# Diagonal matrices of B: made on ScalarE, or fetched from zeros kept in DRAM through ScalarE's own DMA queue

## The chip, the cores and the metric

The kernel runs on one core of one Trainium2 chip. The core has five engines that work side by side, each through its own list of instructions in order: TensorE (PE, matrix products), VectorE (DVE), ScalarE (ACT, functions of single elements and copies), GpSimd (POOL) and SyncE (SP, which here only asks for DMA transfers). Sixteen DMA engines move the data between DRAM and the on-chip memory SBUF. TensorE writes its results to a second on-chip memory, PSUM. The metric is the device time of one execution in microseconds (us). Before the change it is 22,061.91 us, the median of three runs (22,050.39 to 22,083.94).

## The reference: what is computed

Four layers run one after the other on x of shape (4, 64, 64, 128) in float32. Layers 0, 1 and 3 are vision state space layers; layer 2 is a gated block without a scan. Almost all the time goes into the scan of the three state space layers. Cut to what matters, such a layer is:

```python
xz = _ln(input) @ in_proj_w;  x_, z = split(xz)          # 256 channels each
xc = silu(depthwise_conv3x3(x_) + conv_b)                 # B, 256, 64, 64
x0, x1 = rows of xc, columns of xc                        # two orders of the 4096 positions
xs = stack([x0, x1, x0 reversed, x1 reversed])            # K = 4 directions
dts, Bs, Cs = split(einsum('bkdl,kcd->bkcl', xs, x_proj_w), [8, 24])   # R = 8, N = 16, N = 16
delta = softplus(einsum('bkrl,kdr->bkdl', dts, dt_w) + dt_b)
A = -exp(A_log)                                           # K, 256, 16
def step(h, t):                                           # over the 4096 positions
    h = exp(d_t[..., None] * A) * h + (d_t * x_t)[..., None] * B_t[:, :, None, :]
    return h, einsum('bkdn,bkn->bkd', h, C_t)
ys = scan(step) + Ds * xs
y = sum of the four directions, each put back in order
x = input + (_ln(y) * silu(z)) @ out_proj_w
return x + (gelu(_ln(x) @ fc1_w + fc1_b) @ fc2_w + fc2_b)
```

The term (d_t x_t) B_t is what the change touches. For each state n of 16, channel and position it is the product du = delta x of that channel and position with B[n] of that position. B[n] is the same for all channels.

## The kernel before

**Turns, chunks, periods.** Twelve turns (four images, three state space layers) follow one another. A turn has 4 directions of 8 chunks of 512 positions, so there are 384 chunks. Channels lie on the 128 partitions, positions along the rows, and the 256 channels are two halves m. The 16 states are four groups q of CQ = 4. A chunk is worked in eight periods i, one for each pair of group q = i // 2 and half m. There are 3,072 periods.

**A period.** The loop body from L985 on writes the order by hand; nothing reorders it. For its four states a period does four scans on VectorE (L924), each over 512 positions, with the decays da = exp(delta A) from ScalarE (`decay`, L908, for the following period). The input of the scans comes in two ways. The first two states of a group get theirs from TensorE: `pair_db` (L895) multiplies du, transposed to positions on partitions, with a matrix that has B of each position on its diagonal, two states interleaved. The result stands in PSUM as dbp, which has one buffer. The other two states get theirs on VectorE: `lift` (L915) lets ScalarE copy du to PSUM, and L1048 and L1049 multiply it with bb, rows of B that a DMA has spread over all partitions. POOL multiplies the states with C (`times_c`, L936, rows cb spread by DMA), TensorE adds the products up (`add_up`, L951), and ScalarE saves the last states (`save`, L932).

**The diagonals.** `diagonals` (L885) makes the matrices on ScalarE, one half of a group in each period: four activations on the 128 x 128 identity with a column of bt as scale (L891). They are for the group two ahead, or the next chunk's. The tile diag has two buffers of 4 x 128 x 128 x 2 numbers on 128 partitions, 512 KB each. bt is B transposed, from four TensorE transposes (L851) and a ScalarE copy (L856).

**The prologue.** `prologue` (L814) prepares the next chunk in pieces, cut at each `yield`; PIECES says at which half periods the next piece runs: number 2i in the middle of period i, 2i + 1 at its end. The pieces load xs and, for the two reversed directions, xd; project xs to xd (80 rows of dts, B and C for two directions, L835 and L837); project dts to delta (L842, L845) and apply softplus (L847, with loads of function tables); transpose B; store xd to DRAM (L854); form du on POOL (L859) and transpose it (L865, L867).

**SyncE's queue.** All DMA requests are SyncE's, in the order of the program: `spread` (L870) for bb and cb each group, xs, xd, the store of xd, and those of the interleaved steps. A request waits on SyncE until its buffer is free.

**The other layers' work.** `between` makes lists of small steps: output norm, gate, projections, MLP, norms, convolution, and the gated layer. `other` (L1008) puts them into four places of each period, by a planner that spreads their cost (`ROOM`, `cost`, `when`) over a turn. `convolve` and `silu` end in stores of the convolved image to DRAM: x_row by rows (L477) and x_col by columns, the latter in 128 x 64 runs of eight numbers (L472).

Of the kernel before, what the change touches and what calls it, by code (L numbers as in the profile page):

```python
# [13 lines left out]
F32 = mybir.dt.float32  # L14
AF = mybir.ActivationFunctionType
# [7 lines left out]
DI, N, R, K = 256, 16, 8, 4  # L23
NX = R + 2 * N
HID = 4 * C
CH = 512
NCH = L // CH
RPC = CH // W
P = 128
WP = W + 2  # L30

CQ = 4

PAIRED = (0, 2, 4, 6)


PIECES = (0, 3, 4, 6, 8, 9, 10, 11, 12, 13)


_VSS = [  # L40
# [58 lines left out]
def vss_stack_kernel(ctx: ExitStack, tc: tile.TileContext, x: bass.AP, weights, out: bass.AP, n_batch=B, layers=(0, 1, 2, 3)):  # L99
# [6 lines left out]
    nc = tc.nc  # L106

    const = ctx.enter_context(tc.tile_pool(name="const", bufs=1))
    keep = ctx.enter_context(tc.tile_pool(name="keep", bufs=1, space=DRAM))

    ident = const.tile([P, P], F32, name="ident")
# [14 lines left out]
    for i in layers:  # L126
# [14 lines left out]
        t = const.tile([P, small_n + VSS_N - tail_at], F32, name=f"w{i}")  # L141
# [27 lines left out]
    def cols(c):  # L169
        return slice(c * CH, (c + 1) * CH)  # L170
# [13 lines left out]
    y_sb = const.tile([P, 2, L], F32, name="y_sb")  # L184
# [574 lines left out]
        return [S[a:z] for a, z in zip([0] + marks[1:], marks[1:] + [len(S)])]  # L759


    turns = []
    for e in range(0, n_batch, 2):
        for i in (0, 1, 3):
# [2 lines left out]
    for turn, (e, i) in enumerate(turns):  # L767

        for nth, k in enumerate((1, 3, 0, 2) if turn else (0, 1, 3, 2)):
            for ci in range(NCH):  # L770
                s = SimpleNamespace(turn=turn, e=e, v=wt[i], layer=i, nth=nth, k=k, ci=ci)
                s.c = NCH - 1 - ci if k >= 2 else ci
                s.columns, s.back = k % 2 == 1, k >= 2
                s.end = 0 if s.back else CH - 1
                s.step = slice(None, None, -1 if s.back else 1)
                s.first, s.last = ci == 0, ci == NCH - 1
                s.flip = len(chunks) % 2
                s.diag, s.cb, s.bb, s.h, s.hc = {}, {}, {}, {}, {}
                chunks.append(s)
    per_turn = K * NCH  # L780

# [27 lines left out]
    def scans(pool, ring, deep, psum):  # L809
# [4 lines left out]
        def prologue(s):  # L814


            lane, v = lanes[s.e % 2], s.v
            s.xs = ring.tile([P, 2, CH], F32, tag="xs", name="xs")
            nc.sync.dma_start(out=s.xs, in_=(lane.x_col if s.columns else lane.x_row)[:, :, cols(s.c)])
            if s.first:  # L820
                s.dt = pool.tile([R, DI], F32, tag="dt", name="dt_w")
                nc.sync.dma_start(out=s.dt, in_=weights[s.layer][1][:, s.k * DI : (s.k + 1) * DI])


            s.xd_d = lane.xd[s.k % 2][s.c]
            s.xd = pool.tile([2 * NX, CH], F32, tag="xd", name="xd")
            if s.back:
                nc.sync.dma_start(out=s.xd[:NX], in_=s.xd_d[1])
            yield
            if s.back:  # L830
                yield
            else:
                ps = psum.tile([P, CH], F32, tag="misc", name="ps_x")
                for m in range(2):
                    nc.tensor.matmul(ps[: 2 * NX], v["xp"][:, s.k % 2, m, :], s.xs[:, m], start=(m == 0), stop=(m == 1))  # L835
                yield
                nc.scalar.copy(s.xd, ps[: 2 * NX])  # L837
            s.delta = pool.tile([P, 2, CH], F32, tag="delta", name="delta")
            halves = (s.flip, 1 - s.flip)
            for m in halves:  # L840
                ps = psum.tile([P, CH], F32, tag="misc", name="ps_dt")
                nc.tensor.matmul(ps, s.dt[:, m * P : (m + 1) * P], s.xd[:R], start=True, stop=True)  # L842
                yield
                func = AF.Identity if m == halves[0] else AF.Softplus
                nc.scalar.activation(s.delta[:, m], ps, func, bias=v["dtb"][:, s.k, m : m + 1])  # L845
            m = halves[0]
            nc.scalar.activation(s.delta[:, m], s.delta[:, m], AF.Softplus)  # L847
            nc.scalar.preload_act_table_set("natural_log_exp_and_others")
            ps = psum.tile([P, 4, NX], F32, tag="misc", name="ps_bt")
            for j in range(4):  # L850
                nc.tensor.transpose(ps[:, j, :], s.xd[:NX, j * P : (j + 1) * P], ident[:NX, :NX])  # L851
            yield
            if not s.back:
                nc.sync.dma_start(out=s.xd_d.rearrange("k r t -> (k r) t"), in_=s.xd)  # L854
            s.bt = pool.tile([P, 4, N], F32, tag="bt", name="bt")
            nc.scalar.copy(s.bt, ps[:, :, R : R + N])  # L856
            s.du = pool.tile([P, 2, CH], F32, tag="du", name="du")
            for m in halves:
                nc.gpsimd.tensor_mul(s.du[:, m], s.delta[:, m], s.xs[:, m])  # L859
                yield  # L860
            s.duT = pool.tile([P, 4, 2, P], F32, tag="duT", name="duT")
            for m in halves:
                ps = psum.tile([P, 4, P], F32, tag="misc", name="ps_duT")
                for j in range(4):
                    nc.tensor.transpose(ps[:, j, :], s.du[:, m, j * P : (j + 1) * P], ident)  # L865
                yield
                nc.scalar.copy(s.duT[:, :, m, :], ps)  # L867
            yield

        def spread(s, q, b):  # L870

            rows_of, at, count = ((s.bb, CQ * q + 2, CQ - 2), (s.cb, CQ * q, CQ))[b]
            rows_of[q] = pool.tile([P, count, CH], F32, tag="bc"[b] + "b", name="bc"[b] + "b")
            row = R + b * N + at
            nc.sync.dma_start(
                out=rows_of[q], in_=s.xd_d[s.k // 2 : s.k // 2 + 1, row : row + count].to_broadcast([P, count, CH])
            )
# [4 lines left out]
            q = i // 2  # L882
            return q, (i + q + s.flip) % 2

        def diagonals(s, q, half):  # L885

            if half == 0:
                s.diag[q] = pool.tile([P, 4, P, 2], F32, tag="diag", name="diag")
            for t in (2 * half, 2 * half + 1):
                for j in range(2):  # L890
                    nc.scalar.activation(  # L891
                        s.diag[q][:, t, :, j], ident, AF.Copy, scale=s.bt[:, t, CQ * q + j : CQ * q + j + 1]
                    )

        def pair_db(s, i):  # L895
            q, m = place(s, i)
# [6 lines left out]
        def decay(s, i, side):  # L903
            q, m = place(s, i)
            da = ring.tile([P, 2, CH], F32, tag="da", name="da")
            for j in range(2):
                n = CQ * q + 2 * side + j
                nc.scalar.activation(da[:, j], s.delta[:, m], AF.Exp, scale=s.v["a"][:, s.k, m, n : n + 1])  # L908
            return da
# [5 lines left out]
        def lift(s, i):  # L915
            nc.scalar.copy(dv[i % 2], s.du[:, place(s, i)[1]])  # L916
# [17 lines left out]
        def times_c(s, i, side):  # L934
            hc = s.hc[i, side] = deep.tile([P, 2, CH], F32, tag="hc", name="hc")
            nc.gpsimd.tensor_mul(hc, s.h[i, side], s.cb[i // 2][:, 2 * side : 2 * side + 2, :])  # L936
            if side == 1 and i in PAIRED:
                nc.gpsimd.tensor_add(hc, hc, s.hc[i, 0])  # L938

        def add_up(s, i, *calls):  # L940
# [4 lines left out]
            for call in calls:  # L945
                opens = i == start and call == (2 if i in PAIRED else 0)
                if opens:
# [21 lines left out]
        for step in sum([combine(0, psums)] + opening[:4], []):  # L969
            step()  # L970
        s = chunks[0]
        pro = prologue(s)
        for _ in pro:
            pass
        for q, half in ((0, 0), (0, 1), (1, 0)):
            diagonals(s, q, half)
        spread(s, 0, 0)
        spread(s, 0, 1)
        pair_db(s, 0)
# [5 lines left out]
        for at, (s, i) in enumerate(periods):  # L985
            then = periods[at + 1] if at + 1 < len(periods) else None
            if i == 0:
                nxt = chunks[at // 8 + 1] if at // 8 + 1 < len(chunks) else None
                if nxt:
                    pro, nxt.dt = prologue(nxt), s.dt  # L990
                s.state = pool.tile([P, 2, N], F32, tag="state", name="state") if s.first else before[0].state
                if at % (8 * per_turn) == 0:
                    segments = [
                        SimpleNamespace(todo=steps, done=0, dense=True, total=len(steps), frm=frm, to=to)

                        if to - frm <= 4 * 8
                        else SimpleNamespace(
                            todo=steps, done=0, dense=False, total=sum(map(cost, steps)), frm=when(frm), to=when(to)
                        )
                        for steps, frm, to in meanwhile(s.turn)  # L1000
                    ]

            def piece(number):

                if nxt and number in PIECES:
                    next(pro)
# [34 lines left out]
            other(1)  # L1041
            if spreads:
                spread(*spreads, 1)
            if then:
                da_next[1] = decay(*then, 1)
            save(s, i, 0)
# [6 lines left out]
            times_c(s, i, 1)  # L1053
            if then:
                lift(*then)

            q, half = (i + 2 + i % 2) // 2, 1 - i % 2
            if q < 4:
                diagonals(s, q, half)
            elif nxt:  # L1060
                diagonals(nxt, q - 4, half)
            if i < 2 and full:
                leave(*full.pop(0))
            if before:
# [107 lines left out]
```

## Time and profile before

One profiled execution took 22,072.22 us; its span is 22,070.4 us and the granted TensorE clock was 0.963 of full speed.

| What | From the page |
|---|---|
| TensorE matmuls | 19,694.9 us, 89% of the span |
| VectorE | 19,479.8 us, 88% |
| GpSimd | 19,266.5 us, 87% |
| ScalarE | 18,587.9 us, 84% |
| Diagonals on ScalarE (L891) | 12,288 activations, 3,952.1 us |
| B transposed: TensorE (L851), ScalarE copy (L856) | 170.5 us, 73.6 us |
| SyncE's DMA queue | 2,436,336 packets, 3,046.22 MB, 44.4% of 16 engines' span |
| DMA, all queues | mean 139 GB/s |

A line of the groups names the line of the kernel, the engine, the operation, out<-in by tile names with shapes, and the count; behind the bar stand busy us, mean ns of one, and the idle time just before them with what ended it. A line of the waits names the engine, line and tile that waited, and for what; then us in total, times and the longest. A timeline line has start, length (both us), engine, line, operation and out<-in; SPq is SyncE's queue of requests, and a length there is how long SyncE was held by the request, not how long the transfer took. A line of the view by windows has the stretch, its length, busy us (and instructions) of PE, PEld (weight loads), DVE, ACT and POOL, the granted clock, the mean busy share of the 16 DMA engines, and GB/s.

### The profile page before, as it was taken

The page shows a single profiled execution, that of the slowest core. Times are in us where ns is not written, and L with a number is a line of the kernel's source. Part 1 is how long each engine was busy: PE and PEld are TensorE (multiplying, and loading weights), DVE is VectorE, ACT ScalarE, POOL GpSimd, SP SyncE. Part 2 cuts the span into 40 slices and gives each one's busy share as a digit, 9 for nine tenths or more (in the row PEclk, how much of TensorE's full clock was granted, in tenths as well). Part 3 has the DMA queues.
Part 4 walks back from the last instruction along what each step waited for, and adds up shares of the span by engine and source line. Part 5 has one row for each costly group of instructions (what it writes and reads, how often), then busy time and mean ns, then how long its engine had stood idle before and what let it go on. Part 6 is the DMA issues. An engine that isn't in the chain of part 4 may idle for free. (4 is left out here: it accounts for less than half of the span.)

```text
span 22070.4 us, 216982 instructions
## 1 busy us (share of the span) xinstructions
PE 19694.9 (89%) x58234; PEld 10511.8 (48%) x58234; DVE 19479.8 (88%) x20186; ACT 18587.9 (84%) x40022; POOL 19266.5 (87%) x8862
## 2 busy tenths in 40 slices
PE   7898998898889889889989988989988988898897
PEld 3444444444444444444444444444444444444443
DVE  5999999999888888899889899989988888889996
ACT  6888888888888888888888888888888888888887
POOL 5999899899888888888889888988988888889996
PEclk9999999999999999999999999999999999999999
DMA  4444444444335434434534544444443453354342
GB/s 109 147 149 146 135 144 149 136 139 151 130 131 139 142 128 140 146 133 145 144 138 144 145 141 140 141 147 134 142 149 127 137 143 137 131 140 145 140 144 101
DMA packets 2437559, 3060.10 MB, mean 139 GB/s; under 512 B 1753840, under 2 KB 1790064, under 8 KB 2238192
## 3 DMA queue, kind: packets, MB, share of 16 engines
q1 hardware_dynamic: 2436336, 3046.22, 44.4%
q8 instruction: 472, 7.73, 0.1%
q14 instruction: 751, 6.15, 0.1%
HBM read 2784.41 MB, written 261.49 MB: 138 GB/s over the span
## 5 line engine op out<-in xcount | busy, mean ns | idle before, releaser
L936 POOL TENSOR_TENSOR hc<-h,cb 128x1024 f32<-128x1024 f32 x6144 | 14399.4, 2363 | 2276.5 <-DVE h L924 1113.1
L951 PE MATMUL yp<-hc,ident 128*128 128x512 f32 x18432 | 9062.1, 618 | 688.3 <-POOL hc L938 546.8
L908 ACT ACTIVATE da<-delta,w 128x512 f32<-128x512 f32 x12288 | 8148.0, 713 | 543.5 <-DVE h L924 530.5
L924 DVE TENSOR_TENSOR_SCAN h<-da,state,dbp 128x512 f32<-128x512 f32 x5376 | 6573.3, 1262 | 818.9 <-PE dbp L899 576.0
L899 PE MATMUL dbp<-diag,duT 128*128 128x256 f32 x24576 | 6012.6, 388 | 652.4 <-DVE h L924 560.1
L924 DVE TENSOR_TENSOR_SCAN h<-da,state,dv 128x512 f32<-128x512 f32 x5376 | 6589.4, 1264 | 0.0
L899 PEld LDWEIGHTS dbp<-diag,duT 128*128 128x128 f32 x24576 | 4675.2, 193 | 2921.3 <-issue 1673.1
L951 PEld LDWEIGHTS yp<-hc,ident 128*128 128x128 f32 x18432 | 3483.6, 196 | 4999.1 <-issue 3656.8
L891 ACT ACTIVATE diag<-ident,bt 128x128 f32<-128x128 f32 x12288 | 3952.1, 402 | 0.0
L938 POOL TENSOR_TENSOR hc<-hc 128x1024 f32<-128x1024 f32 x1536 | 3624.1, 2359 | 120.4
L1048 DVE TENSOR_TENSOR dv<-dv,bb 128x512 f32<-128x512 f32 x3072 | 2088.3, 680 | 945.9 <-ACT dv L916 730.3
L916 ACT COPY dv<-du 128x512 f32<-128x512 f32 x3072 | 1799.1, 586 | 984.6 <-DVE h L924 977.1
L1049 DVE TENSOR_TENSOR dv<-dv,bb 128x512 f32<-128x512 f32 x3072 | 2118.4, 690 | 0.0
L444 PE MATMUL gap<-halo,cw 128*128 128x512 f32 x3456 | 1750.8, 604 | 5.9 <-DVE cen L281 2.2
L924 DVE TENSOR_TENSOR_SCAN h<-da,dbp 128x512 f32<-128x512 f32 x768 | 891.1, 1202 | 250.7 <-PE dbp L899 166.9
L859 POOL TENSOR_TENSOR du<-delta,xs 128x512 f32<-128x512 f32 x768 | 979.9, 1276 | 31.8 <-ACT delta L847 31.8
L842 PE MATMUL ps_dt<-xd,dt_w 8*128 8x512 f32 x1536 | 881.2, 654 | 130.2 <-ACT delta L845 78.2
L932 ACT COPY state<-h 128x2 f32<-128x2 f32 x5376 | 964.3, 179 | 0.0
L444 PEld LDWEIGHTS gap<-halo,cw 128*128 128x128 f32 x3456 | 628.1, 191 | 654.8 <-issue 617.8
L924 DVE TENSOR_TENSOR_SCAN h<-da,dv 128x512 f32<-128x512 f32 x768 | 893.8, 1204 | 0.0
L845 ACT ACTIVATE delta<-ps_dt,w 128x512 f32<-128x512 f32 x768 | 524.9, 683 | 103.0 <-PE ps_dt L842 98.2
L865 PEld LDWEIGHTS ps_duT<-ident,du 128*128 128x128 f32 x3072 | 383.7, 142 | 321.9 <-issue 255.8
(122 smaller groups left out, 11686.6 us busy)
## 6 DMA issues: line engine op xcount, KB each, us to landing
cb<-xd_d SPq DMA_DIRECT2D x1536, 1024.0 KB
bb<-xd_d SPq DMA_DIRECT2D x1536, 512.0 KB
xs<-x_row_d SPq DMA_DIRECT2D x192, 512.0 KB
xs<-x_col_d SPq DMA_DIRECT2D x192, 512.0 KB
x_col_d<-down SPq DMA_DIRECT2D x192, 256.0 KB
x_row_d<-wide SPq DMA_DIRECT2D x96, 512.0 KB
y_d<-y_sb SPq DMA_DIRECT2D x96, 512.0 KB
y<-y_d SPq DMA_DIRECT2D x96, 512.0 KB
```

Source lines behind the costliest of these rows:

```text
L444: nc.tensor.matmul(z.ps, z.cw[:, m, t, :], z.halo[c][:, dy : dy + RPC, dx : dx + W], start=(t == 0), stop=(t == 8),)
L859: nc.gpsimd.tensor_mul(s.du[:, m], s.delta[:, m], s.xs[:, m])
L891: nc.scalar.activation(s.diag[q][:, t, :, j], ident, AF.Copy, scale=s.bt[:, t, CQ * q + j : CQ * q + j + 1])
L899: nc.tensor.matmul(s.db[:, t * P : (t + 1) * P, :], s.duT[:, t, m, :], s.diag[q][:, t], start=True, stop=True)
L908: nc.scalar.activation(da[:, j], s.delta[:, m], AF.Exp, scale=s.v["a"][:, s.k, m, n : n + 1])
L916: nc.scalar.copy(dv[i % 2], s.du[:, place(s, i)[1]])
L924: nc.vector.tensor_tensor_scan(s.h[i, side][:, j, s.step], da[:, j, s.step], db[:, s.step], init, ALU.mult, ALU.add)
L936: nc.gpsimd.tensor_mul(hc, s.h[i, side], s.cb[i // 2][:, 2 * side : 2 * side + 2, :])
L938: nc.gpsimd.tensor_add(hc, hc, s.hc[i, 0])
L951: nc.tensor.matmul(getattr(s, f"yp{m}"), ident, s.hc[i, side][:, j], start=opens, stop=closes)
L1048: nc.vector.tensor_mul(db, du, s.bb[i // 2][:, 0])
L1049: nc.vector.tensor_mul(du, du, s.bb[i // 2][:, 1])
```

## The change

B's diagonal matrices are no longer computed. Two regions of DRAM, one for even and one for odd chunks, are filled with zeros at the start. A region has, for each of the four groups, 512 rows of DIAG = 258 numbers, one row for each position. Once xd of a chunk is there, ScalarE asks for two DMA transfers (j = 0, 1) that write B of the group's first two states into columns 0 and 1 of the rows of all positions: 4 x 512 single numbers each, 258 apart. The reader takes the same memory as rows of 256 numbers instead of 258 (129 rows to each 128 positions, the last left out). Read so, position p's two numbers stand at columns 2p and 2p + 1 of row p: a diagonal. `diagonals` becomes one DMA load of 512 KB for a whole group, also asked for by ScalarE, in the middle of every odd period, for the group that TensorE needs two periods on. The transposes of B and bt go. The store of xd moves from the piece at number 9 to a new piece at number 5, together with the two transfers; the identity and the second product for delta move to number 7. There is one piece more.

```diff
+DIAG = 2 * P + 2
-PIECES = (0, 3, 4, 6, 8, 9, 10, 11, 12, 13)
+PIECES = (0, 3, 4, 5, 7, 8, 9, 10, 11, 12, 13)
...
+    diag_d = []
+    zero = y_sb.rearrange("p m l -> p (m l)")[:, : N // CQ * 4 * DIAG]
+    nc.vector.memset(zero, 0.0)
+    for j in range(2):
+        diag_d.append(keep.tile([N // CQ, CH * DIAG], F32, name=f"diag_d{j}"))
+        nc.sync.dma_start(
+            out=diag_d[j].rearrange("q (p c) -> p q c", p=P), in_=zero.rearrange("p (q c) -> p q c", q=N // CQ)
+        )
...
                 s.flip = len(chunks) % 2
+                s.diag_d = diag_d[s.flip]
...
                 yield
                 nc.scalar.copy(s.xd, ps[: 2 * NX])
+            yield
+            if not s.back:
+                nc.sync.dma_start(out=s.xd_d.rearrange("k r t -> (k r) t"), in_=s.xd)
+            rows = s.diag_d.rearrange("q (t c) -> q t c", c=DIAG)
+            for j in range(2):
+                nc.scalar.dma_start(out=rows[:, :, j], in_=s.xd[R + j : R + N : CQ])
...
             nc.scalar.preload_act_table_set("natural_log_exp_and_others")
-            ps = psum.tile([P, 4, NX], F32, tag="misc", name="ps_bt")
-            for j in range(4):
-                nc.tensor.transpose(ps[:, j, :], s.xd[:NX, j * P : (j + 1) * P], ident[:NX, :NX])
             yield
-            if not s.back:
-                nc.sync.dma_start(out=s.xd_d.rearrange("k r t -> (k r) t"), in_=s.xd)
-            s.bt = pool.tile([P, 4, N], F32, tag="bt", name="bt")
-            nc.scalar.copy(s.bt, ps[:, :, R : R + N])
...
-        def diagonals(s, q, half):
-
-            if half == 0:
-                s.diag[q] = pool.tile([P, 4, P, 2], F32, tag="diag", name="diag")
-            for t in (2 * half, 2 * half + 1):
-                for j in range(2):
-                    nc.scalar.activation(
-                        s.diag[q][:, t, :, j], ident, AF.Copy, scale=s.bt[:, t, CQ * q + j : CQ * q + j + 1]
-                    )
+        def diagonals(s, q):
+            s.diag[q] = pool.tile([P, 4, P, 2], F32, tag="diag", name="diag")
+            nc.scalar.dma_start(
+                out=s.diag[q].rearrange("p t c n -> p t (c n)"),
+                in_=s.diag_d[q].rearrange("(t p c) -> p t c", t=4, c=2 * P)[:P],
+            )
...
-        for q, half in ((0, 0), (0, 1), (1, 0)):
-            diagonals(s, q, half)
+        for q in range(2):
+            diagonals(s, q)
...
             if spreads:
                 spread(*spreads, 1)
+
+            if i % 2:
+                q = i // 2 + 2
+                if q < 4:
+                    diagonals(s, q)
+                elif nxt:
+                    diagonals(nxt, q - 4)
             if then:
                 da_next[1] = decay(*then, 1)
...
             if then:
                 lift(*then)
-
-            q, half = (i + 2 + i % 2) // 2, 1 - i % 2
-            if q < 4:
-                diagonals(s, q, half)
-            elif nxt:
-                diagonals(nxt, q - 4, half)
```

## The prediction, made before the changed kernel had run

> **What bounds the kernel now.** The page's first part was read first, to see whether one engine sets the time.
>
> ```profile
> PE 19694.9 (89%) x58234; PEld 10511.8 (48%) x58234; DVE 19479.8 (88%) x20186; ACT 18587.9 (84%) x40022; POOL 19266.5 (87%) x8862
> ```
>
> None does. Four engines are 84 to 89% busy and wait for one another, so the groups come next, for what ScalarE would lose and what a chunk costs at least.
>
> ```profile
> L936 POOL TENSOR_TENSOR hc<-h,cb 128x1024 f32<-128x1024 f32 x6144 | 14399.4, 2363 | 2276.5 <-DVE h L924 1113.1
> L908 ACT ACTIVATE da<-delta,w 128x512 f32<-128x512 f32 x12288 | 8148.0, 713 | 543.5 <-DVE h L924 530.5
> L891 ACT ACTIVATE diag<-ident,bt 128x128 f32<-128x128 f32 x12288 | 3952.1, 402 | 0.0
> L938 POOL TENSOR_TENSOR hc<-hc 128x1024 f32<-128x1024 f32 x1536 | 3624.1, 2359 | 120.4
> L859 POOL TENSOR_TENSOR du<-delta,xs 128x512 f32<-128x512 f32 x768 | 979.9, 1276 | 31.8 <-ACT delta L847 31.8
> ```
>
> Over 384 chunks POOL's three groups are 49.5 us a chunk. On VectorE four scans and two products take about 6.2 us a period, 49.6 us a chunk. The span gives 57.5 us a chunk, so some 8 us a chunk are lost to waits. The starts of the scans (L924) in the trace give the mean length of periods 0 to 7: 7.57, 7.31, 7.20, 7.21, 7.41, 7.29, 6.38, 6.46 us. Periods 3 to 5 last 21.9 us together where 18.6 would do: 3.3 us of the loss lies there.
>
> The list of waits says how much of it is ScalarE being late.
>
> ```profile
> ACT dv L916 <- DVE h L924: 977.1, 1124, 4.0
> DVE h L924 <- PE dbp L899: 742.8, 557, 8.6
> DVE dv L1048 <- ACT dv L916: 730.3, 328, 7.5
> POOL hc L936 <- DMA cb<-xd_d: 406.8, 81, 13.0
> DVE dv L1048 <- DMA bb<-xd_d: 196.1, 64, 6.3
> DVE h L924 <- ACT da L908: 104.7, 62, 16.8
> ```
>
> VectorE waits 730.3 + 104.7 = 835 us for ScalarE, 2.2 us a chunk; as often ScalarE is ahead (977 us). Relief of ScalarE is worth at most about that.
>
> Last, what a DMA request costs the engine that makes it: SyncE's own timeline.
>
> ```profile
> 10249.75 0.37 SPq L472 DMA_DIRECT2D x_col_d<-down  x1
> 10250.17 4.50 SPq L477 DMA_DIRECT2D x_row_d<-wide  x1
> 10254.76 0.55 SPq L875 DMA_DIRECT2D cb<-xd_d  x1
> 10255.35 1.02 SPq L472 DMA_DIRECT2D x_col_d<-down  x1
> 10256.47 8.50 SPq L327 DMA_DIRECT2D xt<-in_x  x1
> ```
>
> A request takes 0.3 to 0.5 us, but one made just after the x_col store is held 4.5 us. That store is 128 x 64 runs of 32 bytes, 8,192 pieces. In the trace all 108 requests that directly follow one are held, 4.48 us at the least, 4.54 in the middle. The view by windows shows why:
>
> ```profile
> 10251.00:10252.00 1.00, 0.33 (x1) 0.29 (x2) 1.00 (x2) 1.00 (x3) 1.00 (x1) 1.00 0.76 54
> 10252.00:10253.00 1.00, 1.00 (x3) 0.28 (x2) 0.88 (x1) 1.00 (x2) 0.77 (x1) 1.00 0.76 54
> ```
>
> The last column is GB/s: 54 GB/s in 32-byte pieces are 1.7 pieces a ns, one per 9.4 ns on each of 16 engines, and the next request goes out when most of the 512 pieces of each engine are handed out. SyncE computes nothing, so this costs little today.
>
> **The change, part by part.**
>
> *Taken from ScalarE*: 32 diagonal activations a chunk. The timeline shows four in 1.28 us, so 10.3 us, and the bt copy (0.19 us). From TensorE: four transposes (0.24 us each). Alone this is relief of at most the 2.2 us a chunk above; I take half, 1.1 us (periods 0 to 2, 6 and 7), since the rest lies where the new requests are.
>
> *Added to ScalarE, issue*: six requests a chunk (two scatters, four loads). SyncE's rows of similar shape take 0.32 (cb) to 0.53 us (xs): about 2.7 us.
>
> *Added, the scatter.* Each writes 4 rows of xd, 512 numbers each, 258 numbers apart: 2,048 pieces of 4 bytes. How many DMA engines share them? The trace holds 78,832 four-byte completion packets on SyncE's queue from 5,023 requests. That is exactly 16 each, less 6 for the 192 requests of 40 rows and 8 for the 48 of 8 rows: 40 rows use 10 engines, 8 rows 8. So 4 rows use 4, and 512 pieces fall to each, as deep as an x_col store. Bounds for the hold behind one scatter: 1.1 us (a quarter of 4.5, if all pieces were counted together) and 4.5 us (if depth per engine counts). I take 4.5, being nearest to the row in depth. The second scatter follows the first at once and is held; the next request, the load of diagonals 3 in period 3, is held behind the second.
>
> A walk from the end of period 2 (lift at 0.0, scans of period 3 from 1.3 us), with da pairs at 1.33, lift 0.59, save 0.18, the softplus block of period 4 at 3.9 (0.62 + 0.68 + two table loads of 1.28), two scans 2.45, two products 1.35. Before, with a diagonal block of 1.28 in every period: lift(4) ends at 6.9, lift(5) at 15.7, and VectorE begins period 6 at 20.0, never waiting. After: scatter 1 to 1.0, scatter 2 held to 5.5, da 6.8, save 7.0, the load held until scatter 2 is handed out, 10.4, da 11.7, lift(4) 12.5. VectorE wants it at 9.9 and waits 2.6 us. Then identity, da and softplus block, lift(5) at 20.7 where VectorE is ready at 18.7: another 2.0. Period 6 begins at 24.5, 4.6 us later. If it all falls into the 3.3 us lost there anyway, 1.3 remain; if none, 4.6. I take the middle, 3.0 us a chunk.
>
> *Other traffic during the hold.* The scatter's four engines also serve B and C. Nothing to 4.3 us (9.8 us of handing out at the page's 44.4% load); I take 0.5, as cb is only eight long pieces on an engine.
>
> *Loads of diagonals*: 1,536 of 512 KB, 805 MB, 36 GB/s on 139. Each is asked for two periods (14 us) before TensorE needs it and is about 2 us of transfer by the rates of 340 to 410 GB/s seen while cb lands. Cost nothing; the cover is those 14 us. Should one be late, TensorE's pair_db waits, then the next period's first scan. *Pieces moved*: the xd_d store goes from period 4 to the end of period 2, so spreads wait less for it (79 us now); the dt matmuls lie half a period later, with du still in period 4. Nothing.
>
> *Waits*: a load waits for pair_db to free its buffer, as the activations did, and for both scatters. The first load of the next chunk comes in period 5, some 18 us after scatter 1, against 11 us of handing out and about 2 of landing. Behind it stand da, save and lift, so a late scatter would stop VectorE half a period on.
>
> *Start*: memset, two zero fills of 2.1 MB ahead of the first input and one exposed scatter and load: 25 us (5 to 6 us each at 350 GB/s, the rest as one scatter).
>
> Sum against the profiled execution's 22,072 us: (3.0 + 0.5 - 1.1) x 384 = 922, and 25: 23,019. The median of the runs shown is 10 us below that execution: 23,010.
>
> A rule that speaks against the change: the Trainium skill, "DMA: Bandwidth & Descriptors", section "Issuing engines are not separate DMA queues", says requests from several engines run on the same 16 DMA engines and only issue time is saved. And "Perfetto Trace Analysis", section "DMA Instruction — HWDGE (DVE, Sync)", says one descriptor generator is locked by one sequencer until all is generated; no run here shows two queues. By it, ScalarE would also be held behind SyncE's 96 pairs of x_col stores; an estimate from that page with 6 us each is 580 us of hold, and with half of it passed on the time would be 23,300.
>
> **The rivals.**
>
> *The hold is short, the change pays (faster).* If pieces are handed out at 1.7 a ns whatever the engines, a scatter takes 1.2 us, the walk loses nothing, and relief of 1.1 to 2.2 us a chunk stays: 22,072 + 25 - 420 to 845, middle 21,465. For it: one queue's total rate is all that the windows show. Against: the count of completion packets. It decides where the holds add up to less than about 4.5 us a chunk; mine are 7.
>
> *Four-byte writes are slower.* In the second store of each pair, 32-byte packets took 22 ns, not 7. At 22 ns a scatter takes 11.3 us, the two 22.6 where I have 9.8; the 13 us come on top: 23,010 + 13 x 384 = 28,000. Against: 22 ns was seen only with 16 engines writing.
>
> *The DMA engines become the bound.* The scatters' 1.57 million pieces at 9.4 ns on four engines add 3.7 ms there, 17% of the span; the loads' 786,432 pieces of 1 KB at 60 ns (the mean of the trace's 1 KB packets) on sixteen add 2.9 ms, 13%. With the page's 44.4% these four are 75% busy. For it: cb and bb are late already. Against: their requests are few long pieces and come some 10 us ahead of use. If waits for cb and bb (603 us) double, 23,010 + 600 = 23,610.
>
> **How the numbers follow.** The forecast 0.48 (22,400 to 23,700, from the ends 1.3 and 4.6 of the walk with little or much traffic); the DMA bound 0.10; slow writes 0.10, anything above 24,000; the short hold 0.28; a balance within 0.2% (44 us, about what a measurement can tell) 0.04. Slower together 0.68. The range runs from the better half of the short hold, 21,400, to 24,400, which leaves out the slow writes and a little of the relief.
>
> **What would show it.** Right: two scatter requests a chunk of which the second lasts over 4 us on ScalarE, a load in period 3 held likewise, VectorE's wait for dv (730 us) doubled, periods 3 to 5 above 23 us and periods 0 to 2 shorter. Wrong: requests of 0.5 us throughout and the wait for dv near nothing (the short hold), or loads of period 5 waiting on the scatter (slow writes).

## The result, and the profile after

The changed kernel takes 25,651.18 us (median of four runs, 25,630.51 to 25,680.88) where the kernel before takes 22,059.21 us (four runs): 1.1625 times as long, with a 95% interval of 1.1607 to 1.1644. The forecast was slower, 23,010 us, with a range up to 24,400 us. So the direction held and the size did not: 3,592 us came, 950 were forecast.

The page of the changed kernel, its span, the busy times and the two rows of slices for the clock and the DMA engines:

```profile
span 25643.0 us, 204976 instructions
PE 20388.7 (80%) x56698; PEld 10809.4 (42%) x56698; DVE 19509.9 (76%) x20187; ACT 15198.5 (59%) x27350; POOL 19261.5 (75%) x8862
PEclk8888988888998998998889889889889999988999
DMA  5565556556556555655655655555565565566554
```

ScalarE's busy time fell from 18,588 to 15,199 us, 8.8 us a chunk. VectorE and POOL do what they did within 0.2%, 19,510 and 19,262 us, and now stand still a quarter of the time. The sixteen DMA engines are 50 to 60% busy on average. The list of waits says who waits:

```profile
POOL hc L947 <- DVE h L935: 3873.0, 1523, 15.0
ACT da L919 <- issue: 3470.4, 492, 17.8
PE ps_dt L863 <- ACT delta L866: 2818.8, 372, 23.7
ACT da L919 <- DVE h L935: 2622.3, 2196, 11.9
DVE dv L1066 <- ACT dv L927: 2166.2, 512, 17.7
DVE h L935 <- PE dbp L910: 1601.2, 542, 32.5
POOL hc L947 <- DMA cb<-xd_d: 699.8, 109, 21.3
```

ScalarE stands 3,470 us at "issue" ahead of the decays (da): it waits for no other engine, it is inside its own requests. VectorE's wait for ScalarE's dv has gone from 730 to 2,166 us and its wait for TensorE's dbp from 743 to 1,601. TensorE waits 2,819 us for delta. Before, that wait was small:

```profile
PE ps_dt L842 <- ACT delta L845: 78.2, 52, 4.4
```

The wait for C's rows (cb) rose only from 407 to 700 us.

ScalarE's timeline shows one chunk's requests (ACTq is ScalarE's queue of requests; start, length, line):

```profile
10071.04 0.65 ACTq L858 DMA_DIRECT2D diag_d<-xd  x1
10071.52 0.58 ACT L927 COPY dv<-du 128x512 f32<-128x512 f32 x1
10071.72 8.94 ACTq L858 DMA_DIRECT2D diag_d<-xd  x1
10080.71 1.33 ACT L919 ACTIVATE da<-delta,w 128x512 f32<-128x512 f32 x2 [8.61 <-issue]
...
10082.77 3.87 ACTq L901 DMA_DIRECT2D diag<-diag_d  x1
10086.69 1.33 ACT L919 ACTIVATE da<-delta,w 128x512 f32<-128x512 f32 x2 [3.40 <-issue]
...
10098.84 0.37 ACTq L901 DMA_DIRECT2D diag<-diag_d  x1
```

The first scatter's request takes 0.65 us; the second is held 8.94, and the load of diagonals 3 is held 3.87 behind it. The load after that, with nothing in front, takes 0.37. Over all 384 chunks the second scatter takes 7.58 us on average (4.28 to 17.95), the load behind it 7.03, every other load 0.37. ScalarE is 16.4 us a chunk in its requests, while the activations that had been taken from it make up 10.5 us by their own lines in the page before.

The view by windows for the same two holds shows what the DMA engines move meanwhile. The next to last column is the busy share of the DMA engines, the last one GB/s:

```profile
10071.00:10080.70 9.70, 5.99 (x18) 2.84 (x17) 4.09 (x5) 1.10 (x2) 7.46 (x4) 1.00 0.77 230
10080.70:10086.70 6.00, 1.56 (x4) 0.38 (x2) 3.38 (x4) 2.56 (x6) 3.19 (x2) 0.88 0.47 1
```

During the long hold the engines move 230 GB/s, almost all of it for SyncE's queue; behind it 1 GB/s is left, the pieces of 4 bytes alone.

TensorE and VectorE at the same time:

```profile
10072.67 1.12 PE L863 MATMUL ps_dt<-xd,dt_w 8*128 8x512 f32 x2
...
10089.97 2.07 PE L863 MATMUL ps_dt<-xd,dt_w 8*128 8x512 f32 x2 [7.71 <-ACT delta L866]
...
10095.53 1.89 PE L910 MATMUL dbp<-diag,duT 128*128 128x256 f32 x8
```

```profile
10089.33 0.70 DVE L1066 TENSOR_TENSOR dv<-dv,bb 128x512 f32<-128x512 f32 x1 [1.79 <-ACT dv L927]
...
10097.55 1.28 DVE L935 TENSOR_TENSOR_SCAN h<-da,state,dbp 128x512 f32<-128x512 f32 x1 [4.57 <-PE dbp L910]
```

The second product for delta needs the PSUM bank that the identity activation frees, and this activation stands behind the two held requests on ScalarE. TensorE waits 7.71 us for it, and pair_db, which VectorE's next scan needs, stands behind the product on TensorE. The starts of the scans give the mean period lengths 0 to 7: 7.45, 7.24, 7.08, 9.78, 15.48, 6.49, 6.25, 6.32 us. All of the loss is in periods 3 and 4 (10.6 us a chunk); the others are 1.4 us a chunk shorter together.

### The profile page after: what moved, and what is told of

Its sections match the earlier page's. It is cut to its first block, busy times and chain, and to the rows that moved or that the text cites. A ratio compares the mean times of both kernels' runs of the same rounds, so it can differ in the third digit from the quotient of the medians.

```text
span 25643.0 us, 204976 instructions
## 1 busy us (share of the span) xinstructions
PE 20388.7 (80%) x56698; PEld 10809.4 (42%) x56698; DVE 19509.9 (76%) x20187; ACT 15198.5 (59%) x27350; POOL 19261.5 (75%) x8862
## 5 line engine op out<-in xcount | busy, mean ns | idle before, releaser
L962 PE MATMUL yp<-hc,ident 128*128 128x512 f32 x18432 | 9188.2, 623 | 421.3 <-POOL hc L949 342.5
L910 PE MATMUL dbp<-diag,duT 128*128 128x256 f32 x24576 | 6325.8, 403 | 858.9 <-issue 428.5
L910 PEld LDWEIGHTS dbp<-diag,duT 128*128 128x128 f32 x24576 | 4904.8, 204 | 3467.0 <-issue 2245.5
L962 PEld LDWEIGHTS yp<-hc,ident 128*128 128x128 f32 x18432 | 3558.4, 199 | 4628.0 <-issue 3680.5
L863 PE MATMUL ps_dt<-xd,dt_w 8*128 8x512 f32 x1536 | 1151.7, 838 | 2825.4 <-ACT delta L866 2818.8
L446 PE MATMUL gap<-halo,cw 128*128 128x512 f32 x3456 | 1833.4, 629 | 38.2 <-ACT wide L457 18.1
L863 PEld LDWEIGHTS ps_dt<-xd,dt_w 8*128 8x128 f32 x1536 | 285.9, 231 | 3456.1 <-ACT delta L866 3160.4
L881 ACT COPY duT<-ps_duT 128x512 f32<-128x512 f32 x768 | 445.7, 580 | 180.4 <-PE ps_duT L879 178.2
```

Source lines behind the costliest of these rows:

```text
L446: nc.tensor.matmul(z.ps, z.cw[:, m, t, :], z.halo[c][:, dy : dy + RPC, dx : dx + W], start=(t == 0), stop=(t == 8),)
L910: nc.tensor.matmul(s.db[:, t * P : (t + 1) * P, :], s.duT[:, t, m, :], s.diag[q][:, t], start=True, stop=True)
L962: nc.tensor.matmul(getattr(s, f"yp{m}"), ident, s.hc[i, side][:, j], start=opens, stop=closes)
```

## The experiments

All times are medians, beside runs of the kernel before on the same chip (22,054 to 22,066 us). The first expectation names the theories H, T and C that the others refer to. A diff is against the changed kernel unless the text says otherwise, and `...` stands for lines left out.

**Who asks: scatters from SyncE, loads from ScalarE.**

```diff
-                nc.scalar.dma_start(out=rows[:, :, j], in_=s.xd[R + j : R + N : CQ])
+                nc.sync.dma_start(out=rows[:, :, j], in_=s.xd[R + j : R + N : CQ])
```

> The two scatters of a chunk are asked for by SyncE instead of ScalarE; the loads of the diagonals stay with ScalarE, and the transfers are the same. Theory H (the time went into ScalarE being held by its own requests, in the changed kernel 7.6 us behind the first scatter and 7.0 us behind the second in each chunk): ScalarE's requests take 0.4 us each again and periods 3 and 4 go back to about 7 us; SyncE is held instead and some B and C rows come late: 21,600 to 22,900 us. Rival T (the scatters' 4-byte writes fill four DMA engines and delay every transfer, whoever asks): nothing of the loss goes away, 25,000 us or more. Rival C (TensorE's granted clock, 0.90 where it was 0.96 before, is the cause and comes from the DMA traffic): clock stays near 0.90 and the time above 24,500 us.

Measured: 23,443 us, ratio 1.0626 (1.0610 to 1.0642), 540 us above the span that theory H gave and far below the others'. ScalarE's requests take 0.37 us each. The same bytes move, so rival T (the traffic itself) cannot carry the 2,208 us that went. But the price did not vanish; a part of it is now on SyncE. In the waits of this run:

```profile
DVE dv L1066 <- DMA bb<-xd_d: 1639.2, 314, 18.7
POOL hc L947 <- DMA cb<-xd_d: 1065.0, 172, 22.5
```

SyncE is now held (21.1 us a chunk in its requests, 8.0 before), and the requests for B's and C's rows stand behind. Before, these two waits were 196 and 407 us. The run is still 1,512 us above the kernel without scatters (below); how much of this is SyncE's queue and how much the traffic of the scatters itself was not separated.

**Loads from SyncE, scatters from ScalarE.**

```diff
-            nc.scalar.dma_start(
+            nc.sync.dma_start(
                 out=s.diag[q].rearrange("p t c n -> p t (c n)"),
```

> The loads of the diagonals are asked for by SyncE; the scatters stay with ScalarE. H: the second scatter is held as before, about 7.6 us a chunk, but the load no longer stands behind it on ScalarE, so about half of the hold is gone: 22,800 to 24,000 us. T and C: same transfers, same time, 25,000 us or more.

Measured: 24,028 us, ratio 1.0893 (1.0875 to 1.0911), just outside H's upper end. The second scatter is held 8.90 us on average; the hold of the load is gone from ScalarE. Taking one of the two holds off ScalarE took away 1,623 of the 3,720 us by which the changed kernel exceeds the one without scatters (below).

**Sixteen engines instead of four.** The scatters read the copy of xd in DRAM, positions outermost, behind the identity.

```diff
-            rows = s.diag_d.rearrange("q (t c) -> q t c", c=DIAG)
-            for j in range(2):
-                nc.scalar.dma_start(out=rows[:, :, j], in_=s.xd[R + j : R + N : CQ])
...
                 nc.scalar.activation(s.delta[:, m], ps, func, bias=v["dtb"][:, s.k, m : m + 1])
+                if m == halves[0]:
+                    rows = s.diag_d.rearrange("q (t c) -> t q c", c=DIAG)
+                    b_d = s.xd_d[s.k // 2]
+                    for j in range(2):
+                        nc.scalar.dma_start(
+                            out=rows[:, :, j],
+                            in_=b_d[R + j : R + N : CQ].rearrange("q t -> t q"),
+                        )
```

> The scatters read B from its copy in DRAM in the order of positions first, so that 512 and not 4 is the outer count: each should use 16 DMA engines with 128 pieces on each, not 4 with 512. They are asked for half a period later, behind the identity activation, because they need the copy to have landed. H with a hold that goes by depth for each engine: requests of ScalarE take under 2 us, the relief is left: 21,300 to 22,200 us. H with a hold that goes by the number of pieces alone (2,048 as before): held as in the changed kernel, 24,500 to 26,000 us. T by total pieces rather than by engine: 24,500 us or more too, but with short requests.

Measured: 22,653 us, ratio 1.0268 (1.0252 to 1.0283). No expectation met: the second scatter is still held 3.0 us more than the first (3.59 against 0.55 on average), the load not at all. The count of pieces is the same 2,048, so the hold does not go by the number of pieces alone. At the same place in the program but from SBUF on four engines (below) it is 6.34 us. The source differs too, DRAM against SBUF, so the depth on each engine is the likely reason and not the only possible one; why some 3 us are left stays open. That the engines are sixteen is seen in ScalarE's queue: 1,609,728 four-byte packets are 1,572,864 pieces and 16 completions for each of 2,304 requests. In the changed kernel they are 1,600,512: 4 for each scatter, 16 for each load.

**Scatters alone, on the kernel before.** Diagonals are made on ScalarE as before; the two scatters write to DRAM and nobody reads. The zero fill at the start and the new order of the prologue are in it. The diff is against the kernel before.

```diff
-PIECES = (0, 3, 4, 6, 8, 9, 10, 11, 12, 13)
+PIECES = (0, 3, 4, 5, 7, 8, 9, 10, 11, 12, 13)
...
+            yield
+            if not s.back:
+                nc.sync.dma_start(out=s.xd_d.rearrange("k r t -> (k r) t"), in_=s.xd)
+            rows = s.diag_d.rearrange("q (t c) -> q t c", c=DIAG)
+            for j in range(2):
+                nc.scalar.dma_start(out=rows[:, :, j], in_=s.xd[R + j : R + N : CQ])
```

> The kernel before (diagonals made on ScalarE, nothing loaded), to which only the zero fill, the new order of pieces and the two scatters a chunk from ScalarE are added; nobody reads what they write. H: the second scatter is held 7 to 8 us a chunk, and the request behind it is not there, so the loss is that of the first hold on a ScalarE that has no relief: 24,000 to 25,500 us. T: the scatters delay B and C rows only: 22,100 to 22,700 us. If the loads are what costs: as before, 22,060 us.

Measured: 24,138 us, ratio 1.0939 (1.0923 to 1.0956), in H's span. The second scatter is held 7.81 us. Without relief and without loads two requests a chunk cost some 2,000 us.

**The moved pieces alone.** The same without the scatters; the diff is against the run above.

```diff
-            rows = s.diag_d.rearrange("q (t c) -> q t c", c=DIAG)
-            for j in range(2):
-                nc.scalar.dma_start(out=rows[:, :, j], in_=s.xd[R + j : R + N : CQ])
```

> The kernel before with nothing but the zero fill at the start and the new order of the prologue: the store of xd at the end of period 2, the identity and the second product for delta at the end of period 3. No scatter, no load. If the order costs nothing, as the prediction had it: 22,040 to 22,130 us, and the scatters alone account for all of the run with scatters alone (24,138 us). If the relief was lost to the order: 22,250 us or more.

Measured: 22,177 us, ratio 1.0050 (1.0035 to 1.0065). The new order and the zero fill cost 115 us: between the two expectations, and not nothing. Period 4 grew from 7.41 to 8.14 us, period 5 shrank from 7.29 to 6.95, and the first scan starts 10 us later. The scatters alone are then 24,138 - 22,177 = 1,961 us, 5.1 us a chunk for a hold of 7.8.

**No scatters.** Only the two requests a chunk are taken out of the changed kernel. The loads then fetch zeros, so the output lacks B's part in the first two states of each group.

```diff
-            rows = s.diag_d.rearrange("q (t c) -> q t c", c=DIAG)
-            for j in range(2):
-                nc.scalar.dma_start(out=rows[:, :, j], in_=s.xd[R + j : R + N : CQ])
```

> The changed kernel without the scatters; the loads fetch zeros, so B's part in the first two states of each group is left out of the output. It shows what the relief of ScalarE and the loads are worth by themselves. H: no request of ScalarE is held; the diagonals' 10.3 us of ScalarE a chunk are gone: 21,200 to 21,800 us. If the relief is worth nothing (ScalarE's lateness was only the place where other waits showed): 21,950 to 22,150 us. If the loads themselves collide with B and C: above 22,300 us.

Measured: 21,931 us, ratio 0.9942 (0.9927 to 0.9957), between the expectations. Relief, loads and new order together gain 124 us, 0.3 us a chunk, for 10.5 us of ScalarE's work. The scatters cost 25,651 - 21,931 = 3,720 us.

**Relief alone.** Scatters and loads both go; TensorE multiplies with constant zeros, and the same part of the output is missing.

```diff
...
-            s.diag[q] = pool.tile([P, 4, P, 2], F32, tag="diag", name="diag")
-            nc.scalar.dma_start(
...
+            s.diag[q] = zeros[q % 2]
```

> The kernel of the run without scatters (21,931 us), from which the loads of the diagonals go too: TensorE multiplies with two constant tiles of zeros, so B's part in the first two states of each group is left out of the output. ScalarE asks for nothing. If the 1,536 loads of 512 KB cost nothing, as the prediction had it: 21,900 to 21,960 us. If the loads took back part of the relief, by 512 KB on the DMA engines or by 1.5 us of issue a chunk: 21,500 to 21,800 us.

Measured: 21,833 us, ratio 0.9893 (0.9879 to 0.9908), between the expectations. The loads cost 98 us, give or take some 45 by the two runs' intervals. With the order's 115 us added back, the relief itself is 22,177 - 21,833 = 344 us, 0.9 us a chunk.

ScalarE is only 70% busy here, while the three other engines are as full as before. The busy times of this run:

```profile
PE 19443.8 (89%) x56698; PEld 10404.6 (48%) x56698; DVE 19461.5 (89%) x20189; ACT 15218.6 (70%) x27350; POOL 19240.3 (88%) x8862
```

**Another place: both scatters behind the identity.** As in the run on sixteen engines, but from SBUF.

```diff
                 nc.scalar.activation(s.delta[:, m], ps, func, bias=v["dtb"][:, s.k, m : m + 1])
+                if m == halves[0]:
+                    rows = s.diag_d.rearrange("q (t c) -> q t c", c=DIAG)
+                    for j in range(2):
+                        nc.scalar.dma_start(out=rows[:, :, j], in_=s.xd[R + j : R + N : CQ])
```

> The two scatters, as they are, are asked for behind the identity activation (end of period 3) instead of ahead of the first product for delta (end of period 2). The load of diagonals 3 is then ahead of them, not behind, and TensorE's second product for delta no longer waits for an activation that stands behind them. H: one hold of 7 to 8 us a chunk is left, as in the run with the loads from SyncE (24,028 us), and TensorE's wait for delta (2,819 us in the changed kernel) goes: 23,000 to 24,200 us. If the place does not matter: 25,600 us.

Measured: 23,527 us, ratio 1.0667 (1.0649 to 1.0685). This is in H's span. The load of diagonals 3 stands in front and takes 0.37 us, the second scatter is held 6.34. TensorE's wait for delta is down to 154 us; VectorE's for dv (1,414 us, 552 times) remains. 2,124 us less for the same transfers.

**The two scatters apart.**

```diff
             rows = s.diag_d.rearrange("q (t c) -> q t c", c=DIAG)
-            for j in range(2):
-                nc.scalar.dma_start(out=rows[:, :, j], in_=s.xd[R + j : R + N : CQ])
+            nc.scalar.dma_start(out=rows[:, :, 0], in_=s.xd[R : R + N : CQ])
...
                 nc.scalar.activation(s.delta[:, m], ps, func, bias=v["dtb"][:, s.k, m : m + 1])
+                if m == halves[0]:
+                    nc.scalar.dma_start(out=rows[:, :, 1], in_=s.xd[R + 1 : R + N : CQ])
```

> The two scatters, still 512 pieces on each of four engines, are asked for half a period or more apart: the first at the end of period 2, the second behind the identity at the end of period 3, with the load of diagonals 3 between. H: the second finds the first handed out and takes 0.6 us; only the load between is held by the rest of the first, 1 to 5 us a chunk: 22,200 to 23,300 us. T: the same transfers, the same time: 25,000 us or more.

Measured: 22,881 us, ratio 1.0374 (1.0359 to 1.0390), as H had it. The second scatter takes 0.72 us on average; the load that follows a scatter is held 2.9 us on average, half of these loads not at all and a tenth over 8.5 us.

**Sixteen engines and apart.** As in the run on sixteen engines, but the second scatter goes behind the softplus block.

```diff
+                    nc.scalar.dma_start(out=rows[:, :, 0], in_=b_d[R : R + N : CQ].rearrange("q t -> t q"))
...
             nc.scalar.preload_act_table_set("natural_log_exp_and_others")
+            nc.scalar.dma_start(out=rows[:, :, 1], in_=b_d[R + 1 : R + N : CQ].rearrange("q t -> t q"))
             yield
```

> The run on sixteen engines (22,653 us, where the second scatter was still held about 2.9 us a chunk), with the second scatter asked for in the middle of period 4, behind the softplus block. H: both requests take about 0.55 us and the time comes near that of the kernel without scatters: 21,500 to 22,300 us. If the 2.9 us of hold were not what kept it slow: 22,600 us as before.

Measured: 22,150 us, ratio 1.0042 (1.0027 to 1.0057), in H's span. The requests take 0.56 and 0.91 us on average. 3,501 us of the 3,720 that the scatters cost are gone, with every piece of 4 bytes still written. A new wait is left on ScalarE, behind a load that has to wait until the scatter has landed:

```profile
ACT da L921 <- DMA diag_d<-xd_d: 215.6, 65, 8.0
```

**The same with the pieces in their old places.** The diff is against the run above.

```diff
-PIECES = (0, 3, 4, 5, 7, 8, 9, 10, 11, 12, 13)
+PIECES = (0, 3, 4, 6, 8, 9, 10, 11, 12, 13)
...
-            yield
             if not s.back:
```

> The run on sixteen engines with the scatters apart (22,150 us), with the pieces back in the places of the kernel before, less the transposes: store of xd in the middle of period 2, identity and first scatter at period 3, softplus and second scatter in period 4. If the order of the pieces cost the remaining 0.4%: 21,900 to 22,050 us, a little faster than the kernel before. If the rest is the scatter's own traffic and its landing: 22,100 to 22,250 us.

Measured: 22,297 us, ratio 1.0102 (1.0087 to 1.0117): slower, and above both expectations. The loads behind a scatter are held 1.8 us on average, where in the run above they took 0.37. Undoing the order gained nothing when the requests then stood nearer to each other. No version with all of the work in it beat the kernel before.

**Busy instead of held.** There is no scatter, so the same part of the output is missing; ScalarE copies a scratch tile for 7.7 us in their place and for 7.0 us ahead of the load of diagonals 3.

```diff
...
+            for j in range(24):
+                nc.scalar.activation(scratch, ident, AF.Copy, scale=1.0)
             s.delta = pool.tile([P, 2, CH], F32, tag="delta", name="delta")
...
+                if i == 3:
+                    for j in range(22):
+                        nc.scalar.activation(scratch, ident, AF.Copy, scale=1.0)
```

> The run without scatters, where ScalarE works on nothing instead of being held: 24 activations on a scratch tile (0.32 us each, 7.7 us) in the place of the scatters and 22 (7.0 us) ahead of the load of diagonals 3. H: being late is what costs, whatever makes ScalarE late; the time is that of the changed kernel within a few per cent, 25,000 to 26,200 us, with periods 3 and 4 long and TensorE waiting for delta. If the scatters' traffic was a good part of the loss: 23,000 to 24,500 us.

Measured: 26,635 us, ratio 1.2070 (1.2050 to 1.2090), more even than H's span. ScalarE's busy time is 13.9 us a chunk above the run without scatters, near the 14.6 us of the two holds. The waits are those of the changed kernel, with the scatters' traffic gone:

```profile
POOL hc L948 <- DVE h L936: 4713.3, 1602, 14.7
PE ps_dt L864 <- ACT delta L867: 3648.5, 384, 19.4
DVE dv L1070 <- ACT dv L928: 2887.3, 518, 13.8
DVE h L936 <- PE dbp L911: 1628.8, 508, 26.3
```

Its clock and the share of the DMA engines, in slices:

```profile
PEclk8888888888888888888888888888888888888888
DMA  4454445445445435534544544444453444454443
```

ScalarE being late at these two places is enough for all of the loss. That it comes out 984 us above the changed kernel fits the difference that a hold ends at a fixed moment, however late ScalarE arrives, while work is always added; this was not tested. It also settles rival C: the clock falls to 0.88 with the DMA engines about as busy as before the change (mean 145 GB/s, 139 before). So the lower clock follows from the waits and is not what starts them. What the slower clock adds on top was not separated; TensorE's busy time is 20,389 us in the changed kernel and 19,695 before.

The runs with the relief in order of ScalarE's time in its requests (the runs with scatters alone and with moved pieces alone have none, and busy instead of held is left out):

| Kernel | us a chunk in requests | us | ratio |
|---|---|---|---|
| relief alone | 0 | 21,833 | 0.9893 |
| no scatters | 1.5 | 21,931 | 0.9942 |
| scatters from SyncE (SyncE held instead) | 1.5 | 23,443 | 1.0626 |
| sixteen engines, apart | 2.9 | 22,150 | 1.0042 |
| the same, old places | 5.4 | 22,297 | 1.0102 |
| sixteen engines | 5.6 | 22,653 | 1.0268 |
| apart | 7.9 | 22,881 | 1.0374 |
| behind the identity | 8.4 | 23,527 | 1.0667 |
| loads from SyncE | 9.5 | 24,028 | 1.0893 |
| the change | 16.4 | 25,651 | 1.1625 |

From the run without scatters to the change, 14.9 us more in requests make 9.7 us a chunk: two thirds come through. The order is kept by all but the run with the scatters from SyncE, where the hold is on another engine.

## Why the prediction was right in direction and wrong in size

- **The mechanism held.** The four-engine count, the free first scatter, the held second one and the load held behind it came as walked. The bare hold was 4.5 us by the row of the x_col store; it is 4.28 at the least. The start's 25 us came too: the first scan is at 190.4 us instead of 165.5.
- **The step that failed is "Other traffic during the hold", taken as 0.5 us between 0 and 4.3.** In the changed kernel's trace the second scatter's hold contains 3.6 us of SyncE's longer pieces on average (packets over 32 bytes, their times shared out over the sixteen engines): cb 1.6, bb 1.4, xs 0.4 and little else. As a straight line over the 384 chunks, the hold is 4.24 us + 0.94 times that time (correlation 0.92). A longer hold takes in more traffic, so part of this is built in. But it shows in the first 4.28 us of each hold too, the least that any lasts: 81 scatters with less than a tenth of them taken by SyncE's queue were held 4.4 us on average, 239 with more than half 9.2. So the first hold is 7.6 us instead of 4.5, and the load behind is held 7.0 instead of 3.3. Together that is 14.6 us a chunk where the walk had 7.8: 6.8 us more, above even the bound of 4.3. The argument "cb is only eight long pieces on an engine" fails by the trace before the change: cb's packets of 8 KB took 0.353 us each, so eight are 2.8 us, and bb's eight of 4 KB, at 0.198 us, are 1.6 more. That these rows lengthen the hold is read from the trace; no run took them away.
- **The second failure is the halving of the walk.** It gave 4.6 us, of which 3.0 were taken because part would fall into waits that were there. Walked again with the measured holds (second scatter done at 8.6, load at 17.1, lift(4) at 19.3, lift(5) at 27.5) period 6 begins 11.3 us late; periods 3 to 5 grew by 31.75 - 21.91 = 9.8. Most of it came through.
- **A path that the walk lacked**: TensorE's second product for delta behind the held identity, 2,819 us of waits, with pair_db behind it. The waits of VectorE that were foreseen (dv) tripled rather than doubled. The run with the scatters behind the identity took this path away, together with the load's hold, and was 2,124 us faster. The run with the loads from SyncE has no hold of the load on ScalarE either and keeps much of the path (TensorE waits 1,262 us for delta there); it was 1,623 us faster. The 501 us between the two also hold a second scatter's hold that is 2.6 us shorter, so the path alone was not separated.
- **Relief, 1.1 us a chunk**: 0.9 alone (344 us), near. **The loads, nothing**: 98 us. **Moved pieces, nothing**: 115 us. Each of these two zeros was 0.3 us a chunk too small; together they ate two thirds of the relief. Of the 2.7 us of issue that the prediction priced, its sum has only what the walk has; the other loads' 0.37 us each are in the 98 us.
- **Rivals.** The short hold is refuted by the holds themselves. Slow four-byte writes: a hold of 4.4 us where the other queue was quiet leaves no room for 22 ns a piece, which would be 11.3 us. The 22 ns was also too high as a reading: in the trace before, the 32-byte packets of the second stores took 15.7 ns on average and 11 in the middle. The four-byte packets took 9 ns in the middle and 16 on average on four engines, 9.4 on sixteen; why the mean is higher on four stays open. DMA engines as the bound: 57% busy on average, and the four that take the scatters some 76% by an estimate from the packets' times, if SyncE's share is even. With the same scatters asked for by SyncE 2,208 us of the loss were gone, and with ScalarE late and no scatters at all the loss was there.
- **The rule weighed from the Trainium skill**: by "Perfetto Trace Analysis", "DMA Instruction — HWDGE (DVE, Sync)", the generator is locked by one sequencer until all is generated. The trace doesn't show that between the two queues: some 860 requests of SyncE fell into the time in which the scatters were handed out and took 0.32 us in the middle, no more than elsewhere (0.37). The other rule, "DMA: Bandwidth & Descriptors", "Issuing engines are not separate DMA queues", says that asking from several engines saves only issue time, usually small beside the transfer. Here it was not small, and the wrong way round: 14.6 us a chunk of it were put on an engine that computes.

## What to carry to other kernels

Price a DMA request by the pieces that it leaves on each engine, and by what is asked for right after it on the same queue. Here the second request paid for the first, and on a computing engine everything behind it waited. Count which engines it uses (the completion packets show it), and add the time of the other queue's pieces, which the trace has. Before moving work off an engine, ask whether the others are as full: 10.5 us a chunk taken from ScalarE were worth 0.9.

## What the runs showed of the hardware

- A request of 2,048 single numbers from four partitions runs on 4 DMA engines, from 512 rows on 16 (4 and 16 completion packets for each request).
- The next request on that queue, asked for at once behind 512 pieces on each of four engines, is held 4.28 us at the least, 4.4 where the other queue is quiet, and 7.58 on average beside 3.6 us of the other queue's longer pieces. SyncE's requests meanwhile went out in 0.32 us: the other queue was not held.
- Writes of 4 bytes, 1,032 bytes apart, took 9 ns in the middle, like those of 32 bytes; the means on four engines are 16 and on sixteen 9.4, against 12.5 for 32 bytes.
- TensorE's granted clock falls when TensorE waits: 0.963 before (TensorE 89% busy), 0.897 in the changed kernel (80%), 0.88 (77%) with ScalarE busy on nothing, no scatters and 145 GB/s of DMA traffic (139 before). The Trainium skill, "TensorE: Matmul & The Clock Gate", "Part 1: The HAM clock gate", says that the clock is released by recent activity, and these runs agree.
